# The order of a feed-forward layer, taken from the scheduler and written out by hand

## The chip, the cores and the metric

The program runs on one core of a Trainium2 chip. A core has five engines with a queue of their own, each strictly in order: TensorE (PE in the profile, with PEld for its weight loads), VectorE (DVE), ScalarE (ACT), GpSimd (POOL) and SyncE (SP), which here only issues DMAs. The metric is the device time of one execution in microseconds; 3971.81 is the median of three runs before the change, from 3965.83 to 3977.78.

## The reference

The input x has 4 batches of 512 rows and 512 columns, float32. The program computes

```
x = x + 0.5 * ffn(layernorm(x))
x = x + attention(layernorm(x))
x = x + 0.5 * ffn(layernorm(x))
```

ffn is a gated layer with an inner size of 2048: silu(x G) * (x U), multiplied by D. G, U and D are not given as matrices: each is a cubic spline through some 8000 control points, read off at 1048576 samples. Both calls of ffn use the same control points. The attention is a gated delta rule with 32 heads; the change does not touch it.

## The kernel before

Because neighbouring weights lie on one cubic, the kernel does not multiply by G and U directly. A batch goes through these stages (P is 128, names and lines are those of the profile):

- *Features.* The four row tiles of a batch are normalised: statistics on DVE (L297, L298), the power -0.5 on POOL (`ln_rstd`, L302), the product on DVE (`ln_xn`, L305). They are transposed on PE (`ln_pt`, L308) and copied by ACT (L309). Eight matmuls with `lag` (`pf`, L343) give values at nodes; ACT copies each into `fs` (L345; three buffers, shared with the sums below) and SP cuts it in four and spreads it over the eight tiles `ft` (L347). That is 32 transfers of 64 KB a batch.
- *Gate and up* (`hidden`). For 16 blocks of 128 inner columns: two matmuls, `pg` and `pu` (L389), silu on ACT (`ffn_sg`, L391), the product on DVE (`ffn_it`, L393, four buffers), and a write to a DRAM tensor `hid` on SP (L394). `pg` and `pu` share two PSUM buffers.
- *Gather.* The down-projection needs the inner rows in another order. POOL issues 16 indirect DMAs that read rows of `hid` by an index list into 16 tiles `nat` (L400; 24 buffers). `hid` exists twice, for even and odd batches, and a gather needs all of its batch's rows to be written.
- *Projection.* Four sums (`pm`, L414: four matmuls of 32 output rows each, beside each other in the array) are copied by ACT into `fs` (L416) and spread by SP into two tiles `fm` (L419, 16 transfers of 32 KB). Then four PSUM tiles `y` accumulate: the rest (`we`, L424, four matmuls), the totals (`cm` with `fm`, L427, eight) and the blocks (`wr`, L431, 63 matmuls of 32 contracted rows, four beside each other). ACT copies y into `yg` (L436), PE transposes it back (`y_pt`, L439), and DVE adds it to the residual `ffn_xr` in 44 small pieces that undo a permutation of the columns (L458). SP stores the batch (L460).

Every float32 matmul shows as two instructions in the trace. The transposes show as one.

In the first layer the weights are built as well: `block(k)` makes parts of `wc`, `wr`, `we` and `cm` between the gate and up matmuls of batch 0. The second layer loads them.

What sets the order: the feed-forward layers are traced stage by stage, and a scheduler reorders the traced instructions on each engine by priority (earlier in the program is higher) and by when it estimates them ready. So a stage of one batch can slip into gaps of another, and instructions that are traced late (a batch's statistics, or the attention's set-up loads and constants) can be issued early. The attention is written differently: it stands in a `tc.manual_schedule` block, within which PE, DVE, ACT and POOL keep the order of the program; only SP stays with the scheduler. There a calendar delays a step by a number of ticks, so that its consumer is traced after other work.

Of the kernel before, what the change touches and what calls it, by code (L numbers as in the profile page):

```python
# [9 lines left out]
F32 = mybir.dt.float32  # L10
BF16 = mybir.dt.bfloat16
AF = mybir.ActivationFunctionType
ALU = mybir.AluOpType
# [4 lines left out]
P = 128  # L18
S = 512
H = 512  # L20
INTER = 2048
NT = S // P
NC = H // P
NB = INTER // P
DK = 128
LN_EPS = 1e-5
# [236 lines left out]
def tile_macaron(ctx, tc, x, w_qkvz, w_ba, conv_w, dt_bias, a_log, norm_w, w_out, cps, consts, grid, starts, out):  # L263
# [27 lines left out]
    def layer_norm_t(xt, xnT, pools, ps, tag):  # L291

        sm, wk = pools
        mv = sm.tile([P, NT, 2], F32, name="ln_mv")
        for t in range(NT):
            st = sm.tile([P, 6], F32, name="ln_st")
            nc.vector.bn_stats(st, xt[:, t, :])  # L297
            nc.vector.bn_aggr(mv[:, t, :], st)  # L298
        var = sm.tile([P, NT], F32, name="ln_var")
        nc.vector.tensor_scalar(var, mv[:, :, 1], LN_EPS, None, ALU.add)  # L300
        rstd = sm.tile([P, NT], F32, name="ln_rstd")
        nc.gpsimd.tensor_tensor(rstd, var, phalf[:, :NT], ALU.pow)  # L302
        for t in range(NT):
            xn = wk.tile([P, H], F32, name="ln_xn")
            nc.vector.tensor_scalar(xn, xt[:, t, :], mv[:, t, 0:1], rstd[:, t : t + 1], ALU.subtract, ALU.mult)  # L305
            pt = ps.tile([P, NC, P], F32, name="ln_pt", tag=tag)
            for c in range(NC):
                nc.tensor.transpose(pt[:, c, :], xn[:, c * P : (c + 1) * P], ident)  # L308
            nc.scalar.copy(xnT[:, :, t * P : (t + 1) * P], pt)  # L309

# [6 lines left out]
    def ffn(src, dst, build):  # L317
        with ExitStack() as st:
# [10 lines left out]

            def load(b, name, pool):  # L330
                xt = pool.tile([P, NT, H], F32, name=name)
                nc.sync.dma_start(xt, src(b).rearrange("(t p) h -> p t h", p=P))
                return xt

            def features(xt):

                xnT = io.tile([P, NC, S], F32, name="ffn_xnT")
                layer_norm_t(xt, xnT, (sm, wk), ps, "tp")
                ft = [fp.tile([P, S], F32, name="ft") for _ in range(NG_F)]
                for hf in range(2):  # L340
                    for c in range(NC):
                        pf = ps.tile([P, S], F32, name="pf", tag="tp")
                        nc.tensor.matmul(pf, lag[:, c, hf * P : (hf + 1) * P], xnT[:, c, :], start=True, stop=True)  # L343
                        fs = wk.tile([P, S], F32, name="fs", tag="fs", bufs=3)
                        nc.scalar.copy(fs, pf)  # L345
                        for q in range(4):
                            nc.sync.dma_start(  # L347
                                ft[4 * hf + q][NODES * c : NODES * (c + 1)], fs[NODES * q : NODES * (q + 1)]
                            )
                return ft  # L350
# [4 lines left out]
            if build:  # L355
                with ExitStack() as scratch:
                    coefficients, block = spline_weights(built, scratch, wc, ps)
                    ft = features(xt)
                    for f in coefficients:
                        f()  # L360
            else:
                for g in range(NG_F):
                    nc.sync.dma_start(wc[g].rearrange("p m i -> p (m i)"), wg_d[g])
                ft = features(xt)
# [14 lines left out]
            def hidden(b, ft):  # L379

                to = hid[b % 2]
                for k in range(NB):
                    if build and b == 0:
                        block(k, wr, we, cm)
                    pg = ps.tile([P, S], F32, name="pg", tag="gu")
                    pu = ps.tile([P, S], F32, name="pu", tag="gu")
                    at = (k % 2) * P
                    for m, pm in enumerate((pg, pu)):
                        nc.tensor.matmul(pm, wc[k // 2][:, m, at : at + P], ft[k // 2], start=True, stop=True)  # L389
# [6 lines left out]
            def gather(b, np_):  # L396
                to, nat = hid[b % 2], []
                for v in range(NB):
# [6 lines left out]
                return nat  # L405

            def project(b, nat, np_):
                xr = load(b, "ffn_xr", ip)

                fm = [np_.tile([P, S], F32, name="fm", tag="fm", bufs=3) for _ in range(2)]  # L410
                for k in range(4):
# [3 lines left out]
                    fs = wk.tile([P, S], F32, name="fs", tag="fs", bufs=3)  # L415
                    nc.scalar.copy(fs, pf)  # L416
                    for j in range(4):
                        at = 16 * (4 * (k % 2) + j)
                        nc.sync.dma_start(fm[k // 2][at : at + 16], fs[BLK * j : BLK * j + 16])  # L419
# [1085 lines left out]
```

## Time and profile before

| what | us |
| --- | --- |
| median of three runs | 3971.81 |
| the profiled execution | 3967.6 |
| its span | 3965.6 |
| first layer, start to last store issued | 0 to 444.5 |
| second layer, first load of x to the end | 3576.8 to 3965.6 |
| one gather: start of the first to end of the last DMA_INDIRECT | 19.8 to 24.0 |
| one DMA_INDIRECT, and the distance to the next | 0.95, 1.25 |
| ln_rstd on POOL | 1.0 |
| multiply ffn_it on DVE, silu on ACT, a copy on ACT | 0.69, 0.60, 0.58 |

A row of the timeline gives the start from the beginning of the span, the time from the first start to the last end of the merged instructions, the engine, the line, the operation, output and inputs, shapes, the count, and in brackets how long the engine sat idle before and what ended that. "issue" there means that the engine waited for nothing that the profile shows. The chain of work that ended last counts only the part of each instruction that the next had to wait for; a matmul of 512 columns at full clock is 0.43 in it and 0.59 in the timeline, which includes the drain. The granted clock is the share of TensorE's full clock; between 3570 and the end it lies between 0.5 and 1.0.

### The profile page before, as it was taken

What the parts mean: (1) busy time and instruction counts of PE and PEld (TensorE: products, weight loads), DVE (VectorE), ACT (ScalarE), POOL (GpSimd) and SP (SyncE); (2) the same over time, 40 slices, a digit from 0 to 9 for tenths busy, and PEclk for the clock granted to TensorE, in tenths of its full rate; (3) what the DMA queues carried; (4) which work ended last, traced back from release to release, by engine and by line L of the source; (5) the groups of instructions that cost most, each with busy time, mean ns of one, the idle gap of its engine ahead of it and who ended that gap; (6) DMA issues with size and microseconds to landing.
All of it is one profiled execution on the core that took longest, in us unless ns stands there. A gap on an engine that the chain in (4) does not pass through costs nothing. (4 is left out here: it accounts for less than half of the span.)

```text
span 3965.6 us, 62559 instructions
## 1 busy us (share of the span) xinstructions
PE 3618.2 (91%) x24184; PEld 2016.0 (51%) x24184; DVE 2628.9 (66%) x5925; ACT 1471.1 (37%) x3448; POOL 857.8 (22%) x662
## 2 busy tenths in 40 slices
PE   5889559999999999999999999999999999986997
PEld 2333225555555555555555555555555555542333
DVE  5211277887878888878788887787888777533121
ACT  2222113444444444444444444444444444432221
POOL 2122012222222222222222222222222222211111
PEclk7999779999999999999999999999999999978898
DMA  5555211121221222222212121122121121116443
GB/s 177 184 156 153 88 42 54 57 67 58 62 71 57 65 78 59 63 59 63 70 57 85 57 67 58 57 62 71 57 85 58 53 67 54 49 53 205 129 148 107
DMA packets 319191, 323.24 MB, mean 82 GB/s; under 512 B 102736, under 2 KB 237168, under 8 KB 318320
## 3 DMA queue, kind: packets, MB, share of 16 engines
q1 hardware_dynamic: 308656, 285.69, 23.7%
q0 software_dynamic: 10240, 33.56, 2.9%
q8 instruction: 191, 3.13, 0.3%
q14 instruction: 104, 0.85, 0.1%
HBM read 247.60 MB, written 50.59 MB: 75 GB/s over the span
## 5 line engine op out<-in xcount | busy, mean ns | idle before, releaser
L848 DVE SCALAR_TENSOR_TENSOR acc<-pj,cw,acc 128x511 f32<-128x511 f32 (+2 forms) x768 | 573.2, 746 | 150.8 <-ACT acc L846 132.6
L838 PE MATMUL pj<-xnT,w_v 128*128 128x512 f32 x1024 | 521.1, 602 | 0.3 <-ACT gT L1286 0.3
L1301 PE MATMUL py<-w_o,gT 128*128 128x512 f32 x1024 | 513.7, 615 | 0.4
L1153 PE MATMUL pz<-w_z,xnT 128*128 128x512 f32 x1024 | 513.6, 613 | 0.0
L393 DVE TENSOR_TENSOR ffn_it<-pu,ffn_sg 128x512 f32<-128x512 f32 x128 | 88.4, 692 | 292.6 <-PE pu L389 240.7
L838 PE MATMUL pj<-xnT,w_k 128*128 128x512 f32 x512 | 262.5, 621 | 19.9 <-DMA w_k<-in_L_attn_W_qkvz 19.9
L838 PE MATMUL pj<-xnT,w_q 128*128 128x512 f32 x512 | 255.3, 602 | 0.0
L856 ACT ACTIVATE th<-acc 128x512 f32<-128x512 f32 x256 | 163.0, 637 | 236.1 <-DVE acc L848 227.1
L1209 ACT ACTIVATE tq<-pks,rqe 128x128 f32<-128x128 f32 x384 | 120.1, 364 | 340.3 <-DVE rq L1050 198.1
L1279 ACT ACTIVATE oo<-oo,orr 128x128 f32<-128x128 f32 x512 | 162.6, 390 | 207.7 <-POOL oo L1274 207.7
L846 ACT ACTIVATE acc<-pj,cw 128x512 f32<-128x512 f32 x256 | 175.2, 684 | 167.5 <-PE pj L838 166.5
L1301 PEld LDWEIGHTS py<-w_o,gT 128*128 128x128 f32 x1024 | 171.3, 191 | 106.2 <-issue 95.1
L1153 PEld LDWEIGHTS pz<-w_z,xnT 128*128 128x128 f32 x1024 | 169.3, 190 | 99.5 <-issue 88.5
L879 POOL TENSOR_TENSOR rsq<-msq,phalf 128x4 f32<-128x4 f32 x64 | 64.8, 1013 | 684.3 <-DVE msq L877 684.3
L879 POOL TENSOR_TENSOR rsk<-msk,phalf 128x4 f32<-128x4 f32 x64 | 71.3, 1115 | 650.3 <-DVE msk L877 648.7
L838 PEld LDWEIGHTS pj<-xnT,w_v 128*128 128x128 f32 x1024 | 170.7, 191 | 71.0 <-issue 64.1
L400 POOL DMA_INDIRECT nat<-hid,idx x128 | 121.4, 948 | 383.8 <-DMA fm<-fs 279.9
L1035 POOL TENSOR_TENSOR ks<-kn,ws 128x1024 f32<-128x1024 f32 x64 | 122.1, 1908 | 378.7 <-DVE ws L1028 341.7
L860 DVE SCALAR_TENSOR_TENSOR vT<-th,acc 128x512 f32<-128x512 f32 x128 | 182.7, 1427 | 23.6 <-ACT th L856 23.6
L458 DVE TENSOR_TENSOR ffn_xr<-y_pt,ffn_xr 128x96 f32<-128x96 f32 (+6 forms) x352 | 51.4, 238 | 218.7 <-PE y_pt L439 218.7
L960 DVE TENSOR_TENSOR inv<-inv,inv_tmp 128x30 f32<-128x30 f32 (+14 forms) x480 | 168.7, 351 | 16.5
L1267 DVE TENSOR_REDUCE om<-osq 128x4 f32<-128x512 f32 x128 | 87.1, 680 | 137.3 <-ACT osq L1266 137.3
(204 smaller groups left out, 6988.0 us busy)
## 6 DMA issues: line engine op xcount, KB each, us to landing
hid<-ffn_it SPq DMA_DIRECT2D x128, 256.0 KB
w_v<-in_L_attn_W_qkvz SPq DMA_DIRECT2D x64, 512.0 KB
w_z<-in_L_attn_W_qkvz SPq DMA_DIRECT2D x64, 512.0 KB
w_o<-in_L_attn_W_out SPq DMA_DIRECT2D x32, 1024.0 KB
ab<-decay_c SPq DMA_DIRECT2D x64, 512.0 KB
ft<-fs SPq DMA_DIRECT2D x256, 64.0 KB
w_k<-in_L_attn_W_qkvz SPq DMA_DIRECT2D x64, 256.0 KB
w_q<-in_L_attn_W_qkvz SPq DMA_DIRECT2D x64, 256.0 KB
```

The costliest lines, as they stand in the source:

```text
L400: nc.gpsimd.indirect_dma_start(out=nt, out_offset=None, in_=to[:, :], in_offset=bass.IndirectOffsetOnAxis(ap=idx[:, v : v + 1], axis=0),)
L838: nc.tensor.matmul(pj, w()[:, c, col : col + DK], xnT[:, c, :], start=c == 0, stop=c == NC - 1)
L846: nc.scalar.activation(acc, pj, AF.Copy, scale=cw[:, ch, 3:4])
L848: nc.vector.scalar_tensor_tensor(acc[:, d:], pj[:, : S - d], cw[:, ch, 3 - d : 4 - d], acc[:, d:], ALU.mult, ALU.add)
L856: nc.scalar.activation(th, box["acc"], AF.Tanh)
L860: nc.vector.scalar_tensor_tensor(dest(), box["th"], 1.0, box["acc"], ALU.add, ALU.mult)
L879: nc.gpsimd.tensor_tensor(rs, ms, phalf[:, :NT], ALU.pow)
L960: nc.vector.tensor_tensor(ee[:, j + 1 :, :j], ee[:, j + 1 :, :j], tj, ALU.add)
L1035: nc.gpsimd.tensor_tensor(ks, bc(kn, 2, 2), bc(ws, 3, P), ALU.mult)
L1153: nc.tensor.matmul(pz, xnT[:, c, t * P : (t + 1) * P], pair["wz"][:, c].rearrange("p j k -> p (j k)"), start=c == 0, stop=c == NC - 1,)
L1279: nc.scalar.activation(s["oo"][:, t, r], s["oo"][:, t, r], AF.Copy, scale=s["orr"][:, u : u + 1])
L1301: nc.tensor.matmul(box["py"], pair["gT"][r][:, t, :], pair["wo"][:, r, :], start=r == 0, stop=r == 3)
```

## The change

The feed-forward layer is cut into small steps, and the driver at its end writes out their order inside a `tc.manual_schedule` block for PE, DVE, ACT and POOL. Batch 0's gate and up, and the features of batches 0 and 1 (`whole`), stay outside it and are traced as before.

Turn b of the loop holds gate and up of batch b+1 (`main`, 32 steps: one matmul each), the features of batch b+2 (`norms`, `turns`, `inter`), the projection of batch b (`units`, 32 steps) and the transposes back of batch b-1 (`tail`). The 16 gathers of batch b come first. In steps 0 to 3 of `main` stand the four normalisations, the statistics and the power with the first of them. From step 2 to 11 each step of `main` is followed by one or two of the transposes back, the transposes and the feature matmuls. From step 12 on each is followed by two, later one, of the projection's units: sums, blocks, rest, totals, in that order (before: sums, rest, totals, blocks). Turn 2 has no features, and its projection comes after gate and up of batch 3, with the gathers of batch 3 issued between its units. Turn 3 has only the transposes back of batch 2, the projection and the transposes back of batch 3.

A consumer on ACT or DVE is traced one step after its producer on PE (`later(1, ...)`). Buffers: `ln_xn` 3 instead of 2, `fs` 4 instead of 3, `yg` 4 instead of 2, `nat` 20 instead of 24, `fm` 2 instead of 3; `y_pt` takes the PSUM banks of `y` instead of those of the features.

```diff
+            clock, calendar = [0], {}
+            def later(d, f):
+                calendar.setdefault(clock[0] + d, []).append(f)
+            def tick():
+                clock[0] += 1
+                for f in calendar.pop(clock[0], ()):
+                    f()
+            def drain():
+                while calendar:
+                    tick()
...
+            def statistics(xt):
+                mv = sm.tile([P, NT, 2], F32, name="ln_mv")
+                for t in range(NT):
+                    st_ = sm.tile([P, 6], F32, name="ln_st")
+                    nc.vector.bn_stats(st_, xt[:, t, :])
+                    nc.vector.bn_aggr(mv[:, t, :], st_)
+                var = sm.tile([P, NT], F32, name="ln_var")
+                nc.vector.tensor_scalar(var, mv[:, :, 1], LN_EPS, None, ALU.add)
+                rstd = sm.tile([P, NT], F32, name="ln_rstd")
+                nc.gpsimd.tensor_tensor(rstd, var, phalf[:, :NT], ALU.pow)
+                return mv, rstd
             def features(xt):
                 xnT = io.tile([P, NC, S], F32, name="ffn_xnT")
...
                 ft = [fp.tile([P, S], F32, name="ft") for _ in range(NG_F)]
...
+                xn, stat = {}, {}
+                def norm(t):
+                    if t == 0:
+                        stat["mv"], stat["rstd"] = statistics(xt)
+                    mv, rstd = stat["mv"], stat["rstd"]
+                    xn[t] = wk.tile([P, H], F32, name="ln_xn", bufs=3)
+                    nc.vector.tensor_scalar(
+                        xn[t], xt[:, t, :], mv[:, t, 0:1], rstd[:, t : t + 1], ALU.subtract, ALU.mult
+                    )
+                def turn(t):
+                    pt = ps.tile([P, NC, P], F32, name="ln_pt", tag="tp")
                     for c in range(NC):
...
+                        nc.tensor.transpose(pt[:, c, :], xn[t][:, c * P : (c + 1) * P], ident)
+                    later(1, lambda: nc.scalar.copy(xnT[:, :, t * P : (t + 1) * P], pt))
+                def interpolate(hf, c):
+                    pf = ps.tile([P, S], F32, name="pf", tag="tp")
+                    nc.tensor.matmul(pf, lag[:, c, hf * P : (hf + 1) * P], xnT[:, c, :], start=True, stop=True)
+                    def spread():
+                        fs = wk.tile([P, S], F32, name="fs", tag="fs", bufs=4)
                         nc.scalar.copy(fs, pf)
                         for q in range(4):
                             nc.sync.dma_start(
                                 ft[4 * hf + q][NODES * c : NODES * (c + 1)], fs[NODES * q : NODES * (q + 1)]
                             )
+                    later(1, spread)
+                turns = [lambda t=t: turn(t) for t in range(NT)]
+                inter = [lambda hf=hf, c=c: interpolate(hf, c) for hf in range(2) for c in range(NC)]
+                return ft, [lambda t=t: norm(t) for t in range(NT)], turns, inter
+            def whole(xt):
+                ft, norms, turns, inter = features(xt)
+                for n_, t_ in zip(norms, turns):
+                    n_()
+                    t_()
+                    tick()
+                drain()
+                for f in inter:
+                    f()
+                    tick()
+                drain()
                 return ft
...
             def hidden(b, ft):
...
+                to, box = hid[b % 2], {}
+                def gate(k):
                     if build and b == 0:
                         block(k, wr, we, cm)
...
+                    product(k, 0)
+                def product(k, m):
                     at = (k % 2) * P
...
+                    pm = box[m] = ps.tile([P, S], F32, name=("pg", "pu")[m], tag="gu")
+                    nc.tensor.matmul(pm, wc[k // 2][:, m, at : at + P], ft[k // 2], start=True, stop=True)
+                    if m:
+                        pg = box[0]
+                        later(1, lambda: finish(k, pg, pm))
+                def finish(k, pg, pu):
                     sg = wk.tile([P, S], F32, name="ffn_sg")
                     nc.scalar.activation(sg, pg, AF.Silu)
                     it = ip.tile([P, S], F32, name="ffn_it", bufs=4)
                     nc.vector.tensor_tensor(it, pu, sg, ALU.mult)
                     nc.sync.dma_start(to[k * P : (k + 1) * P, :], it)
...
+                return [f for k in range(NB) for f in (lambda k=k: gate(k), lambda k=k: product(k, 1))]
+            def gather(b):
                 to, nat = hid[b % 2], []
...
+                def step(v):
                     nt = np_.tile([P, S], F32, name="nat")
                     nc.gpsimd.indirect_dma_start(
                         out=nt, out_offset=None, in_=to[:, :],
                         in_offset=bass.IndirectOffsetOnAxis(ap=idx[:, v : v + 1], axis=0),
                     )
                     nat.append(nt)
...
+                return nat, [lambda v=v: step(v) for v in range(NB)]
+            def project(b, nat):
+                box = {}
+                own = lambda g: slice(P * g, P * (g + 1))
+                def sums(k):
+                    if k == 0:
+                        box["xr"] = load(b, "ffn_xr", ip)
+                        box["fm"] = [np_.tile([P, S], F32, name="fm", tag="fm", bufs=2) for _ in range(2)]
                     pf = ps.tile([P, S], F32, name="pm", tag="tp")
                     for j in range(4):
                         nc.tensor.matmul(pf[BLK * j : BLK * (j + 1)], pw, nat[4 * k + j], start=True, stop=True)
...
+                    def spread():
+                        fs = wk.tile([P, S], F32, name="fs", tag="fs", bufs=4)
+                        nc.scalar.copy(fs, pf)
+                        for j in range(4):
+                            at = 16 * (4 * (k % 2) + j)
+                            nc.sync.dma_start(box["fm"][k // 2][at : at + 16], fs[BLK * j : BLK * j + 16])
+                    later(1, spread)
+                def blocks(v):
+                    if v == 0:
+                        box["y"] = [py.tile([P, S], F32, name=f"y{g}", tag=f"y{g}") for g in range(4)]
                     for g in range(4 if v < NB - 1 else 3):
                         rows = slice(BLK * g, BLK * (g + 1))
...
+                        nc.tensor.matmul(box["y"][g], wr[rows, v], nat[v][rows], start=v == 0, stop=False)
+                def rest(g):
+                    nc.tensor.matmul(box["y"][g], we[:, own(g)], nat[-1], start=False, stop=False)
+                def total(k, g):
+                    nc.tensor.matmul(box["y"][g], cm[:, k, own(g)], box["fm"][k], start=False, stop=k == 1)
+                    if k:
+                        later(1, lambda: evict(g))
+                def evict(g):
+                    yg = box["yg", g] = wk.tile([P, S], F32, name="yg", tag="yg", bufs=4)
+                    nc.scalar.copy(yg, box["y"][g])
+                def back(g):
+                    pt = py.tile([P, NT, P], F32, name=f"y_pt{g}", tag=f"y{g}")
+                    for t in range(NT):
+                        nc.tensor.transpose(pt[:, t, :], box["yg", g][:, t * P : (t + 1) * P], ident)
+                    for i, f in enumerate(boxes(g, pt)):
+                        later(1 + i // 3, f)
+                    if g == 3:
+                        later(
+                            2 + i // 3,
+                            lambda: nc.sync.dma_start(dst(b).rearrange("(t p) h -> p t h", p=P), box["xr"]),
                         )
...
+                units = [lambda: sums(0), lambda: sums(1), lambda: blocks(0), lambda: sums(2)]
+                units += [lambda v=v: blocks(v) for v in range(1, 4)] + [lambda: sums(3)]
+                units += [lambda v=v: blocks(v) for v in range(4, NB)] + [lambda g=g: rest(g) for g in range(4)]
+                units += [lambda k=k, g=g: total(k, g) for k in range(2) for g in range(4)]
+                return units, [lambda g=g: back(g) for g in range(4)]
+            for f in hidden(0, ft):
+                f()
+                tick()
+            drain()
             built.close()
-            np_ = st.enter_context(tc.tile_pool(name="ffn_nat", bufs=NB + 8))
-            nat = [gather(0, np_)]
-            for b in range(B):
-                if b + 1 < B:
-                    hidden(b + 1, features(load(b + 1, "ffn_x", io)))
-                    nat.append(gather(b + 1, np_))
-                project(b, nat[b], np_)
+            np_ = st.enter_context(tc.tile_pool(name="ffn_nat", bufs=NB + 4))
+            ft = whole(load(1, "ffn_x", io)) if B > 1 else None
+            tail = []
+            with tc.manual_schedule(engines={e.engine for e in (nc.tensor, nc.vector, nc.scalar, nc.gpsimd)}):
+                nat, steps = gather(0)
+                for b in range(B):
+                    for f in steps:
+                        f()
+                    main, norms, turns, inter = [], [], [], []
+                    if b + 1 < B:
+                        main = hidden(b + 1, ft)
+                    if b + 2 < B:
+                        ft, norms, turns, inter = features(load(b + 2, "ffn_x", io))
+                    units, back = project(b, nat)
+                    nat, steps = gather(b + 1)
+                    early = []
+                    for i in range(4):
+                        early += [x for x in (*tail[i : i + 1], *turns[i : i + 1])]
+                    early += inter
+                    lead = 6 * 2
+                    rest_ = units
+                    for i, f in enumerate(main):
+                        for n_ in norms[i : i + 1]:
+                            n_()
+                        f()
+                        tick()
+                        n = -(-len(early) // max(1, lead - i)) if i < lead else 0
+                        if i >= 2 or not turns:
+                            for f in early[:n]:
+                                f()
+                                tick()
+                            early = early[n:]
+                        if i >= lead and b + 2 < B:
+                            n = -(-len(rest_) // (len(main) - i))
+                            for f in rest_[:n]:
+                                f()
+                                tick()
+                            rest_ = rest_[n:]
+                    drain()
+                    for i, f in enumerate(early + rest_):
+                        f()
+                        tick()
+                        for g_ in steps[: 4 if i == 0 else i >= 8] if b + 2 == B else ():
+                            g_()
+                            steps = steps[1:]
+                    tail = back
+                for f in tail:
+                    f()
+                    tick()
+                drain()
```

## The prediction, made before the result was known

> **What bounds the kernel now.** Times in us, from one profiled execution, 3967.6 long with a span of 3965.6; the median of the runs shown is 3971.8, so I add 4.2 at the end. A difference under 0.3% (12 us) cannot be told from no change here.
>
> I read the page first: PE is the busy engine.
>
> ```profile
> span 3965.6 us, 62559 instructions
> PE 3618.2 (91%) x24184; PEld 2016.0 (51%) x24184; DVE 2628.9 (66%) x5925; ACT 1471.1 (37%) x3448; POOL 857.8 (22%) x662
> ```
>
> The share is a mean over the whole; the attention between 445 and 3570 is untouched. So I cut each feed-forward layer in pieces, from batch 1's first gate matmul to the last down-projection matmul: three pieces per layer, broken at the first gate matmul of batches 2 and 3 (stretch, length, then busy and count per engine, granted clock, DMA share, GB/s).
>
> ```profile
> 149.85:243.16 93.31, 83.62 (x303) 34.60 (x302) 19.58 (x64) 20.74 (x36) 19.54 (x21) 0.95 0.48 145
> 243.16:330.91 87.75, 79.91 (x296) 32.47 (x295) 18.46 (x62) 20.73 (x36) 15.13 (x16) 0.95 0.49 151
> 330.91:436.75 105.84, 95.97 (x437) 38.12 (x435) 18.13 (x63) 18.74 (x32) 17.54 (x20) 0.94 0.44 123
> 3650.37:3753.90 103.53, 87.71 (x303) 37.02 (x302) 19.60 (x64) 20.95 (x36) 28.71 (x31) 0.90 0.52 158
> 3753.90:3843.52 89.62, 81.04 (x295) 33.08 (x294) 18.51 (x62) 20.73 (x36) 15.11 (x16) 0.94 0.48 147
> 3843.52:3952.44 108.92, 98.87 (x437) 41.34 (x435) 17.52 (x60) 17.22 (x30) 15.12 (x16) 0.91 0.37 116
> ```
>
> They sum to 589.0 and hold three batches of gate/up, two of features and four projections per layer. PE looks 90% busy, but the timeline of PE shows why that is too kind:
>
> ```profile
> 3740.67 4.73 PE L343 MATMUL pf<-ffn_xnT,lag 128*128 128x512 f32 x10 [0.68 <-ACT ffn_xnT L309]
> 3746.97 1.12 PE L343 MATMUL pf<-ffn_xnT,lag 128*128 128x512 f32 x2 [1.57 <-ACT fs L345]
> 3749.51 2.08 PE L343 MATMUL pf<-ffn_xnT,lag 128*128 128x512 f32 x2 [1.41 <-ACT fs L345]
> ...
> 3799.10 6.73 PE L431 MATMUL y<-nat,wr 32*128 32x512 f32 x56
> 3806.81 1.01 PE L431 MATMUL y<-nat,wr 32*128 32x512 f32 x3 [0.98 <-issue]
> 3808.23 1.83 PE L431 MATMUL y<-nat,wr 32*128 32x512 f32 x4 [0.41 <-issue]
> 3810.36 9.73 PE L431 MATMUL y<-nat,wr 32*128 32x512 f32 x63 [0.30 <-issue]
> ...
> 3929.00 9.50 PE L427 MATMUL y<-fm,cm 128*128 128x512 f32 x16 [5.29 <-DMA fm<-fs]
> 3938.43 14.01 PE L431 MATMUL y<-nat,wr 32*128 32x512 f32 x126
> ```
>
> The reader is to see three losses: features that wait for fs buffers; a block product that takes 14.0 alone but 21 while a gather runs; and a wait for fm (5.3) in the last projection. A fourth is the cadence of gate/up: with two PSUM buffers pu starts are 1.97 apart, for four instructions of 0.43.
>
> **Work.** The chain has 0.86 for each two-instruction matmul, 0.43 each. Per batch: gate/up 64 x 0.43 = 27.5; features 16 x 0.43 + 16 transposes x 0.14 = 9.1; projection: sums 3.7 (32 instructions, 0.115 each), rest 8 x 0.43 = 3.4, totals 16 x 0.43 = 6.9, blocks 14.0, together 28.0; transposes back 2.2. A layer: 3 x 27.5 + 2 x 9.1 + 4 x 28.0 + 3 x 2.2 = 219.3; both 438.6. So 150.4 of 589.0 is idle or slow, and that is all the change can win. Layer starts, batch 0 and the tail after the last matmul (about 13) stay: same instructions in the same order.
>
> **What the new order adds: a stall behind the gathers.** POOL now runs in traced order. Each turn of the batch loop first issues all 16 gathers of batch b; the pow that makes rstd of batch b+2 is traced after them. DVE has norm(0) early in its queue and waits there; the first transpose (PE's fourth or fifth step) waits for norm(0), and so does everything behind it on PE, and on DVE the multiplies that free the gate/up PSUM. The POOL timeline has the price; the second line is such a pow already:
>
> ```profile
> 153.10 0.94 POOL L400 DMA_INDIRECT nat<-hid,idx  x1 [0.30 <-issue]
> 154.06 1.05 POOL L302 TENSOR_TENSOR ln_rstd<-ln_var,phalf 128x4 f32<-128x4 f32 x1
> ...
> 3648.42 1.05 POOL L400 DMA_INDIRECT nat<-hid,idx  x1 [13.14 <-DMA ft<-fs]
> ...
> 3667.28 0.95 POOL L400 DMA_INDIRECT nat<-hid,idx  x1 [0.30 <-issue]
> ```
>
> Batch 0's last pu ended at 3644.86; gathers start 3.6 later, since they need its last hidden rows in DRAM, and end at +23.4; pow 1.0, normalise 0.5, semaphores 0.3: the transpose runs at +25.2. Turn 1: PE has after that pu one unit (0.9), three gate/up matmuls (2.6) and a back transpose (0.6), so it stands 21 in each layer. Turn 0 in layer 2: gate/up of batch 1 starts at 3650.4 as before, ends its three at 3653.0, transpose at 3670.1: 17. Turn 0 in layer 1: 152.5 to 155.8: 3. Turns 2 and 3 have no norms and no such stall. Sum 62. Before, the other pows ran early, as soon as x was in.
>
> **Restart.** After a wait of 7.0 the chain has this:
>
> ```profile
> 3664.61 7.01 issue
> 3671.62 2.07 PE pu L389 x2
> 3673.70 5.63 PE pm L414 x30
> ```
>
> 2.07 against 0.86 and 5.63 against 3.44 is 3.4, with the next group 3.6. The granted clock was 0.50 there. Three long stalls 10.8, the short one 1.5: 12. [...] The rows here show half speed after idles of 1.4 too (2.08 at 3749.51), so before pays it as well; the measured 3.6 is used.
>
> **What it removes.** Features lie among gate/up matmuls, so fs waits are covered by 0.86 of other PE work each; project 0 and 1 of each layer run among gate/up of the next batch, which hides the 1.97 cadence; sums come first and totals last, so the fm wait goes (blocks and rest, 17, cover 16 fm issues of 0.51 plus 2 of landing; uncovered it is 5.3 to 6.0). In the sum these are zeros, less what follows.
>
> **What is left of the losses**, both layers:
> - Batch 3's gate/up has no projection beside it (turn 2): 31.5 against 27.5: 8.
> - Gather of batch 2 under it: between 0 and 13 a layer. 13 is the idle 9.4 and restart 3.6 at 3660 to 3675, where SP had 22 ft transfers ahead of the hidden writes; none here, so 2: 4.
> - Gather of batch 3 under project 2: blocks took 20.8 to 24.5 under a gather, 14.0 without: 0 to 10, taken 7: 14.
> - Row-strip blocks in pairs between full-array matmuls, ten such slots a projection. Bounds 0 and 0.6 a slot. The change from totals to blocks costs 0.16 (3.60 for 8 instructions), a run of sums 0.2 over its rounds: 0.35 x 10 x 4 projections: 14.
> - SP: 32 ft issues took 22.1 at 3742, 2.8 a feature matmul, while PE makes one each 1.7; four fs buffers and the slack behind take most of it. 0 to 12, taken 4.
> - The attention's set-up loads. Before, they went to SP right after the last gate/up (371), one load held SP 16.0 and ACT waited 27.1 for nega until 394.4, with nothing behind it. Now project 2 lies there: its fm transfers and copies queue behind. 0 (if they come later) to 25 (all of it exposed), taken 8, layer 1 only.
> - Resuming and hand-overs, 1 at each of 8 places: 8.
> - Smaller pools (20 nat instead of 24, 2 fm instead of 3): nothing, since a gather now starts after the projection that frees its buffers, and totals end before the next sums copy lands; if that cover failed, 1.25 a gather.
>
> Sum: 438.6 + 62 + 12 + 8 + 4 + 14 + 14 + 4 + 8 + 8 = 572.6, against 589.0: 16 less. 3967.6 - 16.4 + 4.2 = 3955. Own range, by the bounds above: 3930 to 3985.
>
> **Rivals.**
> - *Row strips lose their overlap (slower).* Four strips run side by side only in long runs; cut into groups of 8 to 16 with full-array matmuls between, the blocks go at 0.215 instead of 0.111. For it: where they trickle, three take 1.01 and four 1.83 above. Against: there the feed was late. 126 x 0.104 x 4 = 52 instead of 14: 3994. It decides above 0.75 a slot, where the gain is used up.
> - *No stall.* The pow gets ahead of the gathers, as at 3599.62 before. Then 62 + 12 more are won: 3881. Against: both are POOL instructions, and POOL is in the hand-ordered set.
> - *No change.* Attention set-up and gathers take their upper ends, 17 more and 6 more on project 2: 3978, or 3967 with half of it.
>
> **How the numbers follow.** Forecast 0.45, strips 0.30, no stall 0.12, no change 0.13. Faster by over 12: 0.29 of the forecast, all of no stall, 0.01: 0.42. Within: 0.12 + 0.01 + 0.08 = 0.21. Slower: 0.04 + 0.29 + 0.04 = 0.37. The range leaves out no stall and the upper end of strips: 3920 to 4010.
>
> **What would show it.** On POOL, pow at the end of 16 gathers in turns 0 and 1, and PE idle 17 to 21 before ln_pt in three places, 3 in the first. Granted clock 0.5 after each. pf rows without fs idle. No fm wait before the last totals. Blocks: two units in 1.7 to 2.1 between gate/up matmuls. Wrong if: pow stands first; blocks take over 3 a pair; PE stands elsewhere for over 10, behind ACT waiting for nega above all.

## The result, and the profile after

The changed kernel is slower, by a third of a per cent: 3986.97 us (3980.03 to 3996.93) beside 3972.43 for the kernel before, a ratio of 1.0036 with a 95% interval of 1.0026 to 1.0045. The forecast was 3955, faster; the range of 3920 to 4010 holds the time, the sign is wrong. The profiled execution took 3989.9, with this page:

```profile
span 3988.1 us, 62538 instructions
PE 3608.3 (90%) x24184; PEld 2005.3 (50%) x24184; DVE 2628.2 (66%) x5925; ACT 1472.2 (37%) x3448; POOL 857.1 (21%) x662
```

Instructions and busy time hardly changed, so the loss is idle time. The six stretches, cut at the same places (stretch, length, busy time and count per engine, granted clock, DMA share, GB/s):

```profile
148.13:228.75 80.62, 73.85 (x279) 29.68 (x279) 12.60 (x20) 20.28 (x36) 7.66 (x8) 0.92 0.43 127
228.75:329.82 101.07, 76.47 (x295) 30.49 (x294) 22.56 (x74) 20.39 (x36) 16.24 (x17) 0.85 0.43 130
329.82:453.25 123.43, 110.40 (x463) 42.90 (x462) 24.57 (x108) 20.38 (x34) 33.01 (x36) 0.88 0.47 142
3661.25:3755.08 93.83, 71.76 (x280) 28.23 (x279) 12.60 (x20) 20.29 (x36) 16.41 (x17) 0.87 0.45 138
3755.08:3856.33 101.25, 75.29 (x295) 30.32 (x294) 22.57 (x74) 20.39 (x36) 16.25 (x17) 0.87 0.43 130
3856.33:3975.48 119.15, 107.81 (x463) 42.08 (x462) 23.99 (x105) 18.94 (x32) 30.31 (x32) 0.90 0.44 144
```

They sum to 619.4. Before it was 589.0, and the forecast's sum was 572.6: 47 missed. Outside them 7.9 was won (batch 0 of the second layer 57.2 instead of 61.7, the hand-over to the attention 4.0, the start 1.7, the end 0.5; the attention lost 2.9).

The stall behind the gathers is there. On POOL the power stands behind the sixteenth gather, in all four turns that have features; here the second turn of each layer:

```profile
250.75 0.94 POOL L454 DMA_INDIRECT nat<-hid,idx  x1 [0.30 <-issue]
251.71 1.05 POOL L341 TENSOR_TENSOR ln_rstd<-ln_var,phalf 128x4 f32<-128x4 f32 x1
...
3777.10 0.95 POOL L454 DMA_INDIRECT nat<-hid,idx  x1 [0.30 <-issue]
3778.07 1.04 POOL L341 TENSOR_TENSOR ln_rstd<-ln_var,phalf 128x4 f32<-128x4 f32 x1
```

And PE stands, that is, sits idle, before the first transpose each time (the timeline of PE, idle time in brackets), 66.9 in all, with half speed behind it (2.07 for a pair that takes 1.02):

```profile
158.31 1.97 PE L362 MATMUL ln_pt<-ident,ln_xn 128*128 128x128 f32 x8 [4.70 <-issue]
...
253.49 1.09 PE L362 MATMUL ln_pt<-ident,ln_xn 128*128 128x128 f32 x4 [21.47 <-issue]
254.45 2.07 PE L435 MATMUL pu<-ft,wc 128*128 128x512 f32 x2
...
3683.36 1.97 PE L362 MATMUL ln_pt<-ident,ln_xn 128*128 128x128 f32 x8 [19.28 <-issue]
...
3779.84 1.09 PE L362 MATMUL ln_pt<-ident,ln_xn 128*128 128x128 f32 x4 [21.49 <-DVE ln_xn L355]
```

So the largest term held, and the loss beyond it lies elsewhere. Three more places in the timeline of PE. First, the feature and sum stretch of turn 1, where a silu stands on ACT behind a copy that waits for an `fs` buffer (PE, then ACT):

```profile
3803.43 1.12 PE L435 MATMUL pg<-ft,wc 128*128 128x512 f32 x2 [2.33 <-ACT ffn_sg L442]
...
3811.64 1.13 PE L435 MATMUL pg<-ft,wc 128*128 128x512 f32 x2 [2.00 <-ACT ffn_sg L442]
```

```profile
3802.29 0.59 ACT L371 COPY fs<-pf 128x512 f32<-128x512 f32 x1 [2.38 <-DMA ft<-fs]
3802.77 0.60 ACT L442 ACTIVATE ffn_sg<-pg 128x512 f32<-128x512 f32 x1
```

Second, gate and up of batch 3 beside the gather of batch 2. PE stands with nothing that the profile names, and the pairs behind these stands run at half speed (granted clock 0.64 from 345 to 357):

```profile
345.82 1.12 PE L435 MATMUL pu<-ft,wc 128*128 128x512 f32 x2 [0.56 <-DVE ffn_it L444]
348.48 2.08 PE L435 MATMUL pg<-ft,wc 128*128 128x512 f32 x2 [1.54 <-issue]
352.18 2.08 PE L435 MATMUL pu<-ft,wc 128*128 128x512 f32 x2 [1.62 <-issue]
355.54 2.08 PE L435 MATMUL pg<-ft,wc 128*128 128x512 f32 x2 [1.28 <-issue]
```

Third, the last turn. The first blocks of batch 3's projection wait for the DVE pieces of batch 2, since these read `y_pt` in the banks that the blocks want; the granted clock falls (0.58 from 426 to 431), and 24 block instructions take 4.60 where 2.86 is usual:

```profile
420.19 1.09 PE L491 MATMUL y<-nat,wr 32*128 32x512 f32 x2 [0.61 <-DVE ffn_xr L536]
421.89 2.97 PE L491 MATMUL y<-nat,wr 32*128 32x512 f32 x6 [0.61 <-DVE ffn_xr L536]
...
426.65 4.60 PE L491 MATMUL y<-nat,wr 32*128 32x512 f32 x24
```

Against the sum, both layers: the hidden stage of batch 3 42.9 and 44.4 where 35.7 each was in it (16 more), the last turn 37.3 twice for 31.2 (12), the stall 66.9 for 62 (5), the waits for `fs` some 13 more than their 4. That is 46 of the 47.

### The profile page after: what moved, and what is told of

Same layout as the page of the kernel before. It is cut to its first block, busy times and chain, and to the rows that moved or that the text cites. A ratio compares the mean times of both kernels' runs of the same rounds, so it can differ in the third digit from the quotient of the medians.

```text
span 3988.1 us, 62538 instructions
## 1 busy us (share of the span) xinstructions
PE 3608.3 (90%) x24184; PEld 2005.3 (50%) x24184; DVE 2628.2 (66%) x5925; ACT 1472.2 (37%) x3448; POOL 857.1 (21%) x662
## 5 line engine op out<-in xcount | busy, mean ns | idle before, releaser
L1350 PEld LDWEIGHTS pzz<-rr,tt 128*128 128x128 f32 x768 | 114.9, 193 | 113.3 <-issue 54.5
```

## The experiments

Theory: the order on POOL costs the 67; fs buffers, the banks of `y` and the gather's company cost the rest. Rival: the stands are no matter of order, and come back wherever the work is put. The runs were made on several chips. Every time below stands beside the kernel before on the same chip, and ratios are compared, since chips differ (the kernel before took from 3948 to 3972).

### One repair at a time (a1_pow_first, a2_backs_gu, a3_fs8)

The power first:

```diff
                 for b in range(B):
+                    if b + 2 < B:
+                        xt = load(b + 2, "ffn_x", io)
+                        known = statistics(xt)
                     for f in steps:
                         f()
```

> The load of batch b+2 and its statistics, the power among them, are traced before the 16 gathers of batch b, so that POOL does the power first; nothing else changes. In the changed kernel TensorE stood 4.7, 21.5, 19.3 and 21.5 us before ln_pt (66.9 together), each followed by a stretch at half clock (12 in the prediction's sum for all four). Theory A, the stall is the order on POOL and nothing else: all of it goes, the four turns shorten by 67 + 10 = 77, and the time is 3987 - 77 = 3910, some 62 below the kernel before. Theory B, a running gather also slows the work beside it, as the gate/up matmuls of batch 3 showed (42.9 and 44.4 us instead of 35.7 for the hidden stage beside one): the gathers now lie beside gate/up of batches 1 and 2 and about 8 comes back in three of the four places; turns shorten by 50 to 55, time 3932 to 3937. No gain would mean that TensorE's stand before ln_pt is not caused by POOL: then ln_rstd comes early in the POOL timeline and ln_pt late all the same.

Measured: 3901.94, ratio 0.9881 (0.9864 to 0.9897). The timeline of POOL, and that of PE:

```profile
3696.65 1.04 POOL L341 TENSOR_TENSOR ln_rstd<-ln_var,phalf 128x4 f32<-128x4 f32 x1 [61.63 <-DVE ln_var L339]
3697.89 1.27 POOL L454 DMA_INDIRECT nat<-hid,idx  x1 [0.20 <-issue]
```

```profile
3698.42 1.09 PE L362 MATMUL ln_pt<-ident,ln_xn 128*128 128x128 f32 x4 [2.34 <-DVE ln_xn L355]
```

The power runs ahead of the gathers and PE stands 2.3 instead of 21.5. Turns 0 and 1 took 74.5 and 86.0, and 78.0 and 85.9: against the changed kernel's first profile 6 + 15 + 16 + 15 = 52 less (against a2 and a4, on this chip, the same). Theory B had 50 to 55. Some of what the stall hid came back: PE waited 26 in turns 0 and 1 for copies to `fs` and for silus behind them, where the changed kernel has 12. The longest, 4.3 in turn 1 of each layer, was for a copy that itself waited for `ft` transfers.

The transposes back, in idle banks:

```diff
-                    pt = py.tile([P, NT, P], F32, name=f"y_pt{g}", tag=f"y{g}")
+                    if b == B - 2:
+                        pt = ps.tile([P, NT, P], F32, name="y_ptg", tag="gu")
+                    else:
+                        pt = py.tile([P, NT, P], F32, name=f"y_pt{g}", tag=f"y{g}")
...
+                    if b + 1 == B:
+                        early, rest_ = [], [*units[:2], *tail[:2], *units[2:6], *tail[2:], *units[6:]]
```

> In the last turn the transposes back of batch 2 go into the two PSUM banks of gate and up, which are idle there, instead of the banks of y, and stand between the sums and the first blocks of batch 3's projection. If the last turn (37.3 us in both layers instead of the 31.2 in the sum) is long because the first blocks wait for the DVE pieces that read y_pt in the banks of y: no wait for ffn_xr before y L491, no half clock after it, 31 to 32 us a turn, 11 to 12 less in all, 3975. If it is long for another reason (the clock, instruction issue), 36 to 38 a turn and no change in the time, 3984 to 3990.

Measured: ratio 0.9984 (0.9974 to 0.9993), the last turn 31.0 in both layers. The blocks of the last turn in the timeline of PE, without a wait and at full speed:

```profile
400.88 1.09 PE L511 MATMUL y_ptg<-ident,yg 128*128 128x128 f32 x8
401.90 1.14 PE L491 MATMUL y<-nat,wr 32*128 32x512 f32 x8
...
403.96 2.00 PE L491 MATMUL y<-nat,wr 32*128 32x512 f32 x16
```

The wait for the banks is the cause of the long last turn. (The edit also puts two of the sums ahead of the transposes back; bank and order were not tried apart.)

Eight `fs` buffers (`bufs=8` in both places):

> Eight fs buffers instead of four. In turns 0 and 1 TensorE waits 1.8 to 2.5 us five times for a silu that stands behind copies to fs which wait for ft transfers, with half clock behind the second in a row: some 12 to 14 in all against 4 in the sum. If the buffers are the limit, these waits go: turns 0 and 1 shorten by 12 to 14 in all, 3974. If SP's rate of one ft transfer in 0.62 us is the limit, the hidden writes queue behind 20 to 30 transfers instead of 8, ffn_it (four buffers) runs out, and the wait returns one step later as DVE waiting for hid transfers: 0 to 5 less, 3982 to 3987. The features of batch 1 in layer 1 and 2 (before turn 0) can gain another 3 to 5 each.

Measured: 3935.96, ratio 0.9966 (0.9954 to 0.9979); turn 1 95.3 and 94.1 instead of 100.3 to 101.3 in a2 and a4, turn 0 2 to 4 shorter, 18 in all where 12 to 14 was expected. The matmuls follow each other without a wait (timeline of PE):

```profile
270.58 1.02 PE L367 MATMUL pf<-ffn_xnT,lag 128*128 128x512 f32 x2
271.44 1.02 PE L435 MATMUL pg<-ft,wc 128*128 128x512 f32 x2
```

The buffers were the limit, not SP's rate. In the repaired kernel (c5_fs4 against c3_load, below) the same edit is worth 17.

### Without the gathers (a4_nogather)

```diff
-                    nat, steps = gather(b + 1)
+                    if b == 0:
+                        nat, steps = gather(b + 1)
+                    else:
+                        steps = []
```

> This kernel leaves out the gathers of batches 2 and 3 (32 of 64 in each layer): the projections of batches 2 and 3 read batch 1's gathered rows. The hidden stage of batch 3 took 42.9 and 44.4 us beside the gather of batch 2, and the projection of batch 2 took 43.1 and 37.3 beside the gather of batch 3. If the running gather is what slows them: 32 to 34 (the cadence of two PSUM buffers) and 28 to 29, so 20 to 26 less a layer. If it is something else (the pieces of batch 1 on DVE, the set-up of the attention, hidden writes): 40 or more and 35 or more remain. The last turn, which has no gather beside it, stays at 37.

Measured: 3951.39 in one time, beside 3949.57. Hidden stage of batch 3 34.2 in both layers, projection of batch 2 28.6, last turn 37. The hidden stage in this run, and below it in the changed kernel's first profile:

```profile
330.65:364.81 34.16, 32.78 (x81) 12.33 (x79) 16.82 (x60) 10.14 (x17) 0.00 (x0) 1.00 0.50 180
```

```profile
329.82:372.69 42.87, 36.49 (x82) 13.27 (x80) 16.84 (x60) 10.14 (x17) 15.31 (x16) 0.88 0.69 242
```

So the gather is what slows the hidden stage. But a2 and a3, with the gathers and on this chip, had 39.1 to 39.8 and 28.6 to 33.9, not 42 to 45 and 37 to 43, and no stand named issue: here the gather costs the hidden stage 5 to 6, and the projection in the second layer nothing.

### The chip (r_after, r_before, r_after2)

> The changed kernel once more, unchanged, beside the others on one chip. In the first profile of it the gathers of batches 2 and 3 were accompanied by short stands of all engines that no wait explains (0.4 to 3.3 us, named issue): 345 to 356, 389 to 404, 3874 to 3887, 3915 to 3920. In a1, a2 and a3, which ran on another chip, the same stretches had none of them; there only waits for hidden writes (3.0 to 3.9) and for fm (3.1 to 3.4) were left. If the stands belong to that first chip or execution and not to the kernel: hidden stage of batch 3 39 us (not 42.9, 44.4), projection of batch 2 29 to 34 (not 43.1, 37.3), a sum of windows near 600 instead of 619, the time about 20 under 3987. If they belong to the order of the changed kernel: the same stands again and 619.

> The kernel before, profiled on the same chip. In its first profile the blocks beside a gather took 21 to 24 us instead of 14, with the same stands without a wait. If they belong to the chip: blocks 14 to 15 everywhere here, and the six windows sum to 565 to 575 instead of 589, so that the change loses the same 15 on either chip. If they belong to the kernel: 589 again.

> The changed kernel unchanged. If the chip is of the kind without stands (before near 3950): gate/up of batch 3 39 and projection of batch 2 29 to 34, as in a2 and a3; the ratio is 1.003 again if the kernel before gains as much there, and 0.998 to 1.000 if only the changed kernel gains. On the other kind (before near 3970): 1.003 and 42 to 45, 37 to 48 as before.

On the second chip the changed kernel had the stands again: hidden stage of batch 3 44.8 and 42.0, projection of batch 2 46.3 and 36.6, six stretches of 620.5, 3982.57, ratio 1.0031 (1.0018 to 1.0043). The kernel before has them too, and its stretches are 589.3 again: PE's idle times named issue, those over 0.25 us in the feed-forward layers from 140 us on added up, are 25.1 in its first profile and 19.6 on that chip (19.2 and 20.3 in the changed kernel, its stands behind the power left out). In a1, a2, a3 and a4 they are 2 in all. So they go with the chip and not with the kernel, or with something else that differed between the occasions, since no chip was met twice. r_after2 met one without: the changed kernel 3952.46, the kernel before 3947.99, ratio 1.0010 (0.9999 to 1.0021), stretches that sum to 588. There the long waits in the hidden stage of batch 3 are for hidden writes, once a layer. A write issued between 335 and 358, beside the gather, took 7.1 from issue to landing, one between 258 and 290 took 2.2 (medians). (Timeline of PE, then the stretch, with a DMA share of 1.02 and a granted clock of 1.00:)

```profile
360.47 1.25 PE L435 MATMUL pu<-ft,wc 128*128 128x512 f32 x2 [3.61 <-DVE ffn_it L444]
```

```profile
345.00:357.00 12.00, 11.16 (x24) 3.75 (x22) 3.46 (x5) 3.09 (x6) 5.39 (x6) 1.00 1.02 388
```

A chip with stands costs the kernel before about 21 (3971 against 3950) and the changed kernel about 32 (3985 against 3952). That difference makes most of the 0.36%; without stands 0.1% is left, and its interval (0.9999 to 1.0021) includes no difference at all. The kernel before was not profiled on a chip without stands, so its stretches there are not known.

### All repairs, and the stands (c1_best, c2_it7, c3_load, c5_fs4)

c1 has the three repairs, with the statistics moved into the middle of the turn before, and for batch 3 four banks:

```diff
-                    pm = box[m] = ps.tile([P, S], F32, name=("pg", "pu")[m], tag="gu")
+                    pm = box[m] = ps.tile([P, S], F32, name=("pg", "pu")[m], tag="gu" if b < B - 1 or k % 2 else "tp")
...
+                        if i == 16 and b + 3 < B:
+                            xt = load(b + 3, "ffn_x", io)
+                            known = statistics(xt)
```

> The three repairs together (statistics of a batch in the middle of the turn before, of batch 2 ahead of the gathers; transposes back of batch 2 in the idle banks in the last turn; eight fs buffers), and in the gate/up of batch 3 the four PSUM banks of gate/up and features in turn instead of two. a1 had 535 us in the ten stretches of both layers (74.5, 86.0, 37.5, 33.9, 35.6; 78.0, 85.9, 39.6, 30.4, 33.9). If the repairs add: last turns 31 (8 less), no stand before ln_pt (2.3 twice), no wait for fs in turns 0 and 1 (some 16 less), four banks 4 a layer: about 500 in the stretches, time 3865 to 3870 where a1 had 3902. If the limit under them is SP's one transfer in 0.62 us: 3885 to 3895, with the hidden writes late and DVE waiting for ffn_it.

> As c1_best, and seven ffn_it buffers instead of four. The gate/up of batch 3 stood 3.0 to 3.9 us once in each layer with DVE waiting for a hidden write to land beside the gather. If buffers cure it: 3 to 4 less in each layer and something in turns 0 and 1, 6 to 10 less than c1_best. If the writes are late for good (the DMA rate beside the gather, 400 GB/s): the gather that follows starts no earlier, and nothing is gained over c1_best.

Measured on a chip with stands: 0.9902 (0.9880 to 0.9925) and 0.9898 (0.9881 to 0.9914). The repairs did not add up there, and more `ffn_it` buffers bring nothing. In the second layer the load of x, traced late, landed at 3681 and held DVE, and with it PE for 8.4: c1 itself put that load too late. c3 traces the load at the start of the turn:

> As c1_best, with the load of batch 3's x traced at the start of turn 0 instead of in its middle, where in c1 it went to SP at 3675.11, landed at 3681 and held DVE 17.5 us and TensorE 8.4 us in the second layer. If that is all: turn 0 of the second layer 9 to 10 shorter, 0.2% of the time less than c1 (ratio 0.988 where c1 had 0.990), and more on a chip where the engines do not stand beside the gathers (0.975).

> As c3_load, but with four fs buffers as in the changed kernel. If the fs buffers still matter once the power comes first: waits of 1.6 to 4.3 us for a silu behind fs copies in turns 0 and 1, as a1 had them, and 12 to 20 more than c3_load. If the transfers themselves are late beside the gather: within 5 of it.

Measured, on another chip with stands: c3 0.9892 (0.9874 to 0.9910), turn 0 of the second layer 85.4 where c1 had 93.6; c5 0.9934 (0.9917 to 0.9950). What is left in c3 is above all stands: 50.8 named issue on PE alone, counted as before. The longest, in the timeline of PE and of ACT, which waits for nothing named either:

```profile
3740.93 3.78 PE L367 MATMUL pf<-ffn_xnT,lag 128*128 128x512 f32 x4 [11.15 <-issue]
```

```profile
3740.29 0.59 ACT L363 COPY ffn_xnT<-ln_pt 128x512 f32<-128x512 f32 x1 [11.69 <-remote]
```

### Thinner gathers (c4_paced, p1_paced)

```diff
                     nat.append(nt)
+                    if b < 3:
+                        nc.gpsimd.memset(idle, 0.0)
```

> As c3_load, with a fill of 1024 elements (0.93 us on GpSimd) after each gather of batches 0 to 2, so that a gather goes out every 2.2 us instead of 1.25. If the engines' stands without a wait come from the full DMA engines (share 0.97 to 1.0 and 360 to 420 GB/s in every stretch that has them): they go or halve, the gate/up of batch 3 takes 34 to 36 instead of 41, turns 0 and 1 lose their stands of 2 to 7 us, 15 to 25 less than c3_load. If each indirect transfer itself causes them: as many as before, and no gain. A loss is possible too: 16 gathers take 35 us, and the sums that need the last of them come 30 to 35 us after the first.

> The changed kernel with that fill behind each gather of batch 2 alone. In the changed kernel the gate/up of batch 3 beside that gather took 42.9, 44.4, 44.8 and 42.0 us on two chips, 34.2 without a gather on a third. If the full DMA engines are the cause: 34 to 37, no stand without a wait, and the projection of batch 2 begins by waiting some 3 us for its last gathers. If not: 41 to 45 again.

Measured: c4 3885.06 against 3929.86 for c3, ratio 0.9777 (0.9761 to 0.9794): 45 less through a fill that does no work. The stretch from 10.5 to 22.5 us into turn 1 of the second layer, in c3 (length, busy time and count per engine, clock, DMA share, GB/s):

```profile
3730.00:3742.00 12.00, 1.07 (x2) 0.56 (x3) 1.61 (x10) 0.59 (x1) 9.19 (x10) 0.60 0.79 233
```

and the same work in c4:

```profile
3700.00:3712.00 12.00, 12.00 (x35) 5.02 (x35) 3.48 (x13) 6.18 (x11) 11.01 (x13) 1.00 0.88 282
```

PE is busy 12.0 instead of 1.1, all engines run, and the DMA engines move more. p1, the changed kernel with the fill behind one gather only, in one time on this chip, has the hidden stage of batch 3 at 36.0 and 36.4. Its stretch beside that gather, to be read against that of the changed kernel's first profile below it:

```profile
345.00:357.00 12.00, 11.60 (x24) 3.82 (x23) 3.46 (x5) 3.78 (x7) 10.98 (x13) 1.00 0.98 348
```

```profile
345.00:357.00 12.00, 7.00 (x9) 2.14 (x9) 2.08 (x3) 1.19 (x2) 6.02 (x7) 0.64 0.97 363
```

The DMA share is 0.98 in the one and 0.97 in the other, and it was 1.02 in r_after2 without a stand, so full DMA engines alone are not the cause. What the edit changes is how often GpSimd sends a gather: each 2.1 us or each 1.25. The projection of batch 2, beside the gather of batch 3 that c4 leaves dense, kept its stands there (46.8 and 42.0).

### How thin, and of what kind (c6_paced_all, a6_pow_paced, a4_poolplain, c7_half_fill, c7_again)

> As c4_paced, with the fill after each gather of batch 3 too, which runs beside the projection of batch 2. There c4 had 46.8 and 42.0 us for a projection of 28.6 without a gather beside it (stands without a wait, 349 to 363). If density of issue is the cause there as well: 29 to 32, 10 to 17 less a layer, as long as the 16 gathers (35 us) do not hold up the sums of batch 3: 3860 to 3870 where c4 had 3885. If the blocks, which read the gathered tiles, stand for another reason: no gain, or a loss of up to 10 through the later last gather.

> The changed kernel with two repairs only: the power ahead of the gathers (a1) and the fill after each gather. Without the eight fs buffers, the idle banks for the transposes back and the four banks of gate/up. If the stands beside the gathers were what a1 had left on such chips: turns 0 and 1 76 to 80, gate/up of batch 3 35 to 37, projection of batch 2 29 to 32, last turn 37: 3880 to 3890. If fs buffers are needed too: 3895 to 3905.

> The changed kernel with the gathers of batches 2 and 3 replaced by plain transfers of the same 16 tiles of 256 KB, issued by GpSimd from the same place (rows in order, so the projections of batches 2 and 3 get other rows than they should). If the indirect addressing is what makes the engines stand: the gate/up of batch 3 takes 34 to 37 instead of 42 to 45 and the projection of batch 2 29 to 31 instead of 37 to 48. If it is the load that GpSimd's queue puts on the DMA engines at this density: 42 to 45 and 37 to 48 as before.

> As c6_paced_all, with half the fill (0.5 us, a gather each 1.75 us). If the stands grow steadily with density: half of what pacing won is lost, 3880 to 3895. If there is a rate below which they vanish and 1.75 lies under it: as c6 or 3 to 6 better, since the last gather lands 7 us earlier.

> The version with all repairs and a fill of 0.5 us after each gather, which had a ratio of 0.972 on a chip without stands. On the same kind: 0.972 again. On the other kind: 0.972 to 0.976 if a gather each 1.75 us is thin enough, 0.980 to 0.985 if half of the stands come back (c4, with 0.97 us of fill for three of four gathers, had 0.978 there, c3 without fill 0.989).

Both chips that these met were without stands, so whether plain transfers make them, and whether half the fill is thin enough, stays open.

- c6: 3865.94, ratio 0.9779 (0.9763 to 0.9796).
- a6: 3892.22, ratio 0.9847 (0.9831 to 0.9864), between its two expectations. So fs buffers, banks and the earlier statistics are worth 26 on top of order and fill.
- c7, with a gather each 1.66 us: 3844.40, ratio 0.9723 (0.9705 to 0.9741), and on the other chip 3850.70, ratio 0.9760 (0.9743 to 0.9776). That is 22 less than c6 on one chip, where 3 to 6 was expected: on such a chip the full fill is too much, and in c6 sums wait up to 1.6 for late gathers. No run has all repairs and no fill on such a chip, so what the half fill itself is worth there is not shown.
- a4_poolplain: the hidden stage of batch 3 takes 35.2 and 34.5, with the indirect transfers of r_after2 40.0 and 39.7. This does not single out the index list: beside that stage the plain transfers went out 2.3 to 4.4 us apart in the first layer, some released by a hidden write, and the indirect ones each 1.25.

c7 is the best version measured, 2.4 to 2.8% under the kernel before; on a chip with stands c4 has 2.2%.

## Why the prediction was wrong

The largest term was right. The steps that failed are three small prices in the sum: the gather of batch 2 under gate and up, the `fs` buffers, and the hand-over at the last turn. Term by term:

- *Stall behind the gathers, 62, and restart.* Right: 66.9, in the four places named, and 3.1 lost to the clock at 253 to 260 (granted 0.53 there) where 3.6 was put. Shown by a1. The rival "no stall" put 74 on this order; a1 won 52, since waits for `fs` came back in place of the stall (26 instead of 12).
- *Gather of batch 2 under gate/up, "so 2".* Wrong: without a gather 34.2, with it 39.7 to 40.0 on a chip without stands and 42 to 45 on one with. Between 5 and 11 a layer, inside the bounds of 0 to 13, where 2 was taken. The reason given, that no ft transfers stand ahead of the hidden writes, was not the point: the writes landed late beside the gather (7.1 instead of 2.2 in r_after2; DVE waited for one, and PE 3.0 to 3.9 for DVE, on the chips without stands).
- *Gather of batch 3 under project 2, 14, and the attention's loads, 8.* The two projections of batch 2 were 80 together in the sum and 80.4 measured, by luck. The split was wrong: ACT did wait for nega (15.6 at 394), but only 3.1 to 3.4 of it reached the totals, and in the first profile nothing; the stands beside the gather took the rest. On a chip without stands, r_after2, the two took 33.8 and 28.6, 18 less than the sum.
- *SP and fs buffers, "taken 4".* Mis-sized: 18 by a3 and 17 by c5, above the bound of 12. The sum reckoned that slack on PE covers the wait, but the silus stand behind the copies on ACT, in order (the silu at 3802.77 behind a copy that waited 2.38, and PE 2.33 behind the silu).
- *Resuming and hand-overs, 1 at each place.* The last turn failed here: 5 to 6 a layer. The text noted that `y_pt` moved to the banks of `y` and asked nothing about who wants these banks next. a2 shows it.
- *Row strips.* 0.35 a slot was right. A pair of blocks and a gate/up matmul take 2.99; less 0.86, and 16 instructions at 0.107 to 0.111, that leaves 0.35 to 0.42 (timeline of PE):

```profile
192.91 2.00 PE L491 MATMUL y<-nat,wr 32*128 32x512 f32 x16
194.84 1.13 PE L435 MATMUL pu<-ft,wc 128*128 128x512 f32 x2
195.90 2.00 PE L491 MATMUL y<-nat,wr 32*128 32x512 f32 x16
```

- *The removed losses.* Cadence and fm wait went as said where the order covers them: no fm wait before the totals of turns 0 and 1.

The sign hung on small terms: three of them, each taken near its low end, were 41 short together, against a forecast gain of 16. The blocks at 20.8 to 24.5 under a gather stood in the old trace; on that chip they told that work beside a gather can be slowed, whatever it is.

## What to carry to other kernels

When an order is written by hand, walk each queue, the slow ones first: one small power behind 16 gathers cost 67 us, and tracing it first won 52. For every buffer or bank that changes its pool, ask who wants it next and behind which engine. And a transfer burst may not be free for compute beside it (on one chip, 12 us held 1.07 of PE work beside a gather each 1.25 us, 12.0 beside one each 2.1): where it is not, send it no faster than its reader needs.

## What was not expected of the hardware

Beside gathers that GpSimd issues every 1.25 us, PE, ACT and DVE stand for 0.3 to 11 us with no wait that the profile names: in the first profiles and on two chips met later, and not on three others. The changed kernel itself was profiled on both kinds. A fill of 0.97 us between the gathers removes most of it: 10.7 instead of 50.8 us named issue on PE (c4 and c3, one chip). The mechanism is open. Instruction loading gives no sign in the changed kernel's first profile: its packets of 16 KB take 0.97 us (median of 191), and there is none between 345 and 357, 389 and 404 or 3874 and 3887, where PE stands for up to 1.6, 1.7 and 3.3 beside a gather.

The same 12 us of the changed kernel beside a gather, 345 to 357, held 7.00 of PE work on one chip (363 GB/s) and 11.16 on another (388 GB/s). So a plan that takes a gather as free for the engines was wrong on the first kind of chip.
